# Row broadcasts of attention factors by DMA through DRAM in place of TensorE transposes, with the order picked among 45 candidates

## The chip, the cores and the metric

The kernel runs on one core of one Trainium2 chip. The metric is the device time of one execution in microseconds (us), given as the median of several runs. Each run is marked with a state, fast, slow or unknown: all timed runs told here are fast, and the two probes, which ran once each, unknown. The profile and the trace of one run of each kernel are read beside the times. Engines are PE (TensorE matmuls), PEld (TensorE weight loads), DVE (VectorE), ACT (ScalarE), POOL (GpSimd) and SP (SyncE, which here only issues DMAs). An engine with a "q" behind its name is its queue. A DMA has landed, as the word is used here, when the trace records its semaphore's event. "Granted clock" is the share of its full clock that TensorE has in the records of the profile.

## The reference, cut to what matters

There are 32 batches of `x`, each 512 rows of 256. Each goes through a layer norm, a small MLP, a first attention without a mask, a second MLP, a second attention with the mask `adj`, and then a feed-forward part that does not matter here. Both attentions are of the additive kind:

```python
def _gat(inp, adj_mask, W, a):
    h = jnp.matmul(inp, W)
    F_ = h.shape[-1]
    f1 = jnp.matmul(h, a[:F_, 0])
    f2 = jnp.matmul(h, a[F_:, 0])
    e = jax.nn.leaky_relu(f1[:, :, None] + f2[:, None, :], ALPHA)
    if adj_mask is not None:
        e = jnp.where(adj_mask[None, :, :] > 0, e, NEG_INF)
    att = jax.nn.softmax(e, axis=2)
    h_prime = jnp.einsum('bij,bjf->bif', att, h)
    return jax.nn.elu(h_prime)
```

`f1[i] + f2[j]` needs one of the two vectors as a column, one value per partition, and the other as a row, the same 512 values on all 128 partitions. The matmuls leave both as columns. How the row is made is what the change is about.

## The kernel before

In the first attention the kernel writes exp(leaky_relu(f1 + f2)) as the larger of two products of factors, so only 4 × 512 exponentials are needed (`ex`). Two of the four vectors are needed as rows (`acb`). A column becomes a row by spreading it over 128 columns and transposing that on TensorE, 128 values at a time, into PSUM, from where ScalarE copies it:

```python
        nc.vector.memset(f1, 1.0)
        acb = new("acb", [P, 2, N])
        for s in range(2):
            pt = tr_tile([P, N])
            for i in range(NT):                       # NT = 4, P = 128, N = 512
                nc.tensor.transpose(
                    pt[:, ts(i)], ex[:, s, i : i + 1].to_broadcast([P, P]), ident
                )
            nc.scalar.copy(acb[:, s, :], pt)

        pT = new("pT", [P, NT, N])
        for j in range(NT):
            nc.vector.tensor_scalar(
                pT[:, j, :], acb[:, 1, :], ex[:, 3, j : j + 1], None, op0=OP.mult
            )
            nc.vector.scalar_tensor_tensor(
                pT[:, j, :], acb[:, 0, :], ex[:, 2, j : j + 1], pT[:, j, :],
                op0=OP.mult, op1=OP.max,
            )
        # ... then the matmuls of pT with h ("mm<-h,pT")
```

The second attention does the same with one row, `f2b`, from a column of its `h`, and uses it thus:

```python
            nc.vector.scalar_tensor_tensor(
                e, f2b, h[:, i, D : D + 1], mbias[:, i, :], op0=OP.add, op1=OP.add
            )
            # ... leaky relu, row maximum, exponential, then four transposes of e on TensorE
```

No operation is issued where it is written. A `Recorder` takes all of them, gives each a cost and a lag from a small model of its own, and puts them into one order for each engine, greedily. The front of one batch (to the end of the first attention) runs beside the rest of the batch before. The model's cost of a DMA, which the change leaves as it is:

```python
        if op.method == "dma_start":
            return 0.1, 2.5 + out.size() * 4 / 180e3
```

Of the kernel before, what the change touches and what calls it, by code (L numbers as in the profile page):

```python
# [1 line left out]

# [5 lines left out]

F32 = mybir.dt.float32
# [3 lines left out]
AX = mybir.AxisListType  # L13

ENGINES = ("tensor", "vector", "scalar", "gpsimd", "sync")
LATE, LONG = 1.3, 1.4
P = 128
ALPHA = 0.2
MASKED = -4.5e16
# [2 lines left out]
class Recorder:  # L22



    SIGNAL = 0.16
    DRAIN = 0.17
    KEPT = 1
    AHEAD = 3

    def __init__(self, nc):
        self.nc, self.ops, self.logs, self.age, self.stage = nc, [], {}, -1, 0
# [2 lines left out]

    def _region(self, ap):

        if ap.space == bass.MemoryType.PSUM:
            return 0, P, 1
        (pitch, parts), *rest = ap.ap  # L40
        first, start = divmod(ap.offset, pitch)
        starts, run = [start], 1
        for step, count in rest:
            if step == 1:
                run = count
            elif step:
                starts = [s + step * i for s in starts for i in range(count)]
        bits = 0
        for s in starts:
            for w in range(s // 64, (s + run - 1) // 64 + 1):  # L50
                bits |= 1 << w
        return first, first + parts, bits

    def take(self, engine, method, args, kwargs):
        outs, ins = list(args[:1]), [x for x in args[1:] if isinstance(x, bass.AP)]
        for key, x in kwargs.items():
            if isinstance(x, bass.AP):
                (outs if key in ("out", "accum_out") else ins).append(x)
        op = _Op(engine, method, args, kwargs, self.age, self.stage, len(self.ops))
        op.cost, op.lag = self._cost(op, outs[0], ins)  # L60
        before = {}
        for aps, writes in ((ins, False), (outs, True)):
            for ap in aps:
                if ap.space == bass.MemoryType.DRAM:
                    continue
                lo, hi, bits = self._region(ap)
                log = self.logs.setdefault(ap.tensor.name, _Log(ap, self.age))
                op.logs.add(log)
                kept = []
                for entry in log.entries:  # L70
                    other, olo, ohi, obits, owrites = entry
                    if other is op:
                        kept.append(entry)
                        continue
                    if (writes or owrites) and olo < hi and lo < ohi and obits & bits:
                        before[other.index] = other
                    if not (writes and lo <= olo and ohi <= hi and not obits & ~bits):
                        kept.append(entry)
                kept.append((op, lo, hi, bits, writes))
                log.entries = kept  # L80
        for other in before.values():
            other.after.append(op)
        self.ops.append(op)
# [23 lines left out]
            return (0.1 if op.method == "memset" else 0.3 if op.method == "tensor_scalar" else 1.1), 0.1  # L107
        return 0.2 + n / (480 if op.method == "tensor_tensor" else 960), 0.1

    def _schedule(self, ops, key):  # L110


        free, slots, turn = dict.fromkeys(ENGINES, 0.0), {}, {}
# [32 lines left out]
        while len(done) < len(ops):  # L146
# [23 lines left out]
            for log in op.logs:  # L170
                users[log] -= 1
                until[log] = max(until[log], op.end)
                if not users[log]:
                    slots[log.tag].append(until[log] + self.SIGNAL)
            for later in op.after:
                if later not in left:
                    continue
                if later.engine != op.engine:
                    at = op.end + self.SIGNAL
                else:  # L180
                    at = t + op.cost if op.engine == "tensor" else op.end
                later.ready = max(later.ready, at)
# [6 lines left out]
            done.append(op)  # L189
        return done  # L190

    def order(self):


        work, turns = {}, {}
        for op in self.ops:
            stage = op.age, op.stage
            turns[op] = work.get(stage, 0.0)
            work[stage] = turns[op] + (op.cost if op.engine == "tensor" else 0.0)
        for op in self.ops:  # L200
            part = turns[op] / (work[op.age, op.stage] or 1.0)
            turns[op] = op.age + (LATE + LONG * part if op.stage else part)
        return self._schedule(self.ops, turns.get)

    def emit(self):
        for op in self.order():
# [37 lines left out]
def adj_ffn_kernel(  # L244
# [40 lines left out]
    sbuf = ctx.enter_context(tc.tile_pool(name="sbuf", bufs=1))  # L285
    psum = ctx.enter_context(tc.tile_pool(name="psum", bufs=1, space=bass.MemoryType.PSUM))

    def ts(i, n=P):
        return slice(i * n, (i + 1) * n)

# [8 lines left out]

    def sm_tile(shape):  # L300
        return psum.tile(shape, F32, tag="sm", name="sm", bufs=1)

    def med(name, shape=(P, 4, 256)):
        return new(name, shape, bufs=2, tag="med")
# [211 lines left out]
    def front(b):  # L516
# [48 lines left out]

        nc.vector.memset(f1, 1.0)
        acb = new("acb", [P, 2, N])
        for s in range(2):
            pt = tr_tile([P, N])
            for i in range(NT):  # L570
                nc.tensor.transpose(
                    pt[:, ts(i)], ex[:, s, i : i + 1].to_broadcast([P, P]), ident
                )
            nc.scalar.copy(acb[:, s, :], pt)

        pT = new("pT", [P, NT, N])
        for j in range(NT):
# [27 lines left out]
    def middle(b, o1T):  # L605
# [18 lines left out]
            else:  # L624
                nc.scalar.copy(h[:, t, :], pm)
        f2b = new("f2b", [P, N])
        pt = tr_tile([P, N])
        for j in range(NT):
            nc.tensor.transpose(pt[:, ts(j)], h[:, j, D + 1 : D + 2].to_broadcast([P, P]), ident)
        nc.scalar.copy(f2b, pt)  # L630
        r2 = new("r2", [P, NT, D])
        for t2 in range(NT // 2):
            pt = tr_tile([P, 2, D])
# [249 lines left out]
```

## Time and profile before

| | before |
|---|---|
| median | 3002.47 us (3 runs, 3002.22 to 3004.32) |
| TensorE busy | 98% |
| VectorE, ScalarE busy | 62%, 39% |
| one batch in the middle of the run | 91.28 us |
| granted clock | 0.996 |

TensorE has no time to spare, so the run is the sum of its work. The prediction shows the lines for that. One thing more of the kernel before will be needed, what VectorE waits for when it takes the rows. These are two lines of its groups by shape: busy time in all and mean ns of one, then the idle time just before them and what ended it.

```profile
L207 DVE TENSOR_SCALAR pT<-acb,ex 128x512 f32<-128x512 f32 x128 | 56.1, 481 | 3.5 <-ACT acb L207 3.5
L207 DVE SCALAR_TENSOR_TENSOR e<-f2b,h,mbias 128x512 f32<-128x512 f32 x128 | 92.9, 746 | 2.0 <-PE tr L207 1.7 <-ACT f2b L207 0.4
```

In the whole run VectorE stood idle for 3.5 us before `acb` and for 2.0 us before `e`. The rows came in time.

### The profile page before, as it was taken

To read this page: it belongs to the slowest core of one execution; us is meant where nothing else is said; L and a number is where in the kernel's file an instruction comes from. 1 tells how busy PE (TensorE), PEld (TensorE's weight loads), DVE (VectorE), ACT (ScalarE), POOL (GpSimd) and SP (SyncE) were. 2 spreads that over 40 slices of the span, in tenths; PEclk is the share of its full clock that TensorE was granted. 3 is DMA by queue.
4 is the path that set the end of the run, shared out by engine and by line. 5 is a ranking of instruction groups with operands and counts; after the bars stand their busy time and mean duration, and the time that the engine had idled before them with its cause. 6 is when DMAs were issued, how large, how long until landed. Compare 5 with 4: busy or idle time off the path is not lost.

```text
span 3002.9 us, 35910 instructions
## 1 busy us (share of the span) xinstructions
PE 2942.8 (98%) x13805; PEld 2258.5 (75%) x13805; DVE 1866.3 (62%) x4438; ACT 1174.5 (39%) x2246; POOL 124.6 (4%) x233
## 2 busy tenths in 40 slices
PE   5999999999999999999999999999999999999997
PEld 3777777877777777778777778777777777787775
DVE  3565676655775656666556756557756566665574
ACT  1433444333444334444334443334443344443342
POOL 1000000000000000000000000000000000000000
PEclk9999999999999999999999999999999999999998
DMA  4000000000000000000000000000000000000000
GB/s 130 1 22 1 21 22 22 22 9 13 22 22 22 22 1 22 22 22 22 21 1 22 22 22 22 3 19 22 22 22 22 1 22 22 22 15 13 3 15 14
DMA packets 57410, 58.71 MB, mean 20 GB/s; under 512 B 3988, under 2 KB 55832, under 8 KB 57240
## 3 DMA queue, kind: packets, MB, share of 16 engines
q1 hardware_dynamic: 53904, 54.28, 6.0%
q8 instruction: 110, 1.80, 0.3%
q10 hardware_dynamic: 3336, 2.14, 0.3%
q14 instruction: 60, 0.49, 0.1%
HBM read 39.63 MB, written 16.78 MB: 19 GB/s over the span
## 4 chain that ended last, share of the span: by engine, by line
PE 96%; DVE 2%; DMA 1%; ACT 0%; issue 0%; POOL 0%; SPq 0%; ACTq 0%; POOLq 0%
PE mm L207 84%; PE tr L207 11%; PE sm L207 1%; DVE w L207 1%; DMA wfx<-in_L_ffn_W_fx_dram 0%; DMA temp<-n_L_ffn_temperature_dram 0%; DVE mx L207 0%; DVE rs L207 0%; DVE m L207 0%; DVE u L207 0%; DMA xt<-in_x_dram 0%; ACT m L207 0%; DVE x L207 0%; POOL ln_rstd L207 0%; DVE mbias L207 0%
## 5 line engine op out<-in xcount | busy, mean ns | idle before, releaser
L207 PE MATMUL mm<-wfc,o0T 128*128 128x257 f32 x2048 | 584.5, 383 | 0.0
L207 PE MATMUL mm<-h,pT 128*128 128x256 f32 (+1 forms) x2048 | 523.6, 379 | 0.0
L207 PEld LDWEIGHTS mm<-wfc,o0T 128*128 128x128 f32 x2048 | 363.1, 190 | 117.0 <-issue 83.5
L207 PEld LDWEIGHTS mm<-h,pT 128*128 128x128 f32 x2048 | 379.9, 189 | 63.0 <-issue 13.9
L207 DVE COPY h<-mm 128x257 f32<-128x257 f32 x192 | 81.5, 425 | 378.8 <-PE mm L207 378.8
L207 PE MATMUL mm<-h,p2T 128*128 128x256 f32 x1024 | 292.6, 379 | 0.0
L207 PE MATMUL mm<-gg,wT 128*128 128x256 f32 x1024 | 281.6, 379 | 0.0
L207 PE MATMUL mm<-o1T,w 128*128 128x512 f32 x512 | 262.3, 595 | 0.0
L207 PE MATMUL mm<-xn,w 128*128 128x257 f32 x1024 | 248.2, 380 | 0.0
L207 PE MATMUL mm<-xnT,w 128*128 128x512 f32 x512 | 247.4, 598 | 0.1
L207 PE MATMUL mm<-weff,xn2T 128*128 128x512 f32 x512 | 226.9, 596 | 0.2 <-ACT xn2T L207 0.2
L207 PEld LDWEIGHTS mm<-h,p2T 128*128 128x128 f32 x1024 | 186.5, 189 | 22.7
L207 PEld LDWEIGHTS mm<-xn,w 128*128 128x128 f32 x1024 | 184.6, 190 | 20.9 <-DVE w L207 0.2
L207 PEld LDWEIGHTS mm<-gg,wT 128*128 128x128 f32 x1024 | 179.6, 190 | 17.9 <-ACT gg L207 0.2
L207 PEld LDWEIGHTS mm<-weff,xn2T 128*128 128x128 f32 x512 | 97.9, 192 | 111.0 <-issue 107.9
L207 ACT ACTIVATE w<-w 128x512 f32<-128x512 f32 x128 | 80.6, 630 | 248.0 <-DVE w L207 248.0
L207 ACT ACTIVATE m<-m 128x512 f32<-128x512 f32 x192 | 121.0, 630 | 143.8 <-DVE m L207 140.5
L207 DVE TENSOR_TENSOR w<-mm,beff 128x512 f32<-128x512 f32 x128 | 84.9, 663 | 146.1 <-PE mm L207 146.1
L207 ACT COPY h<-mm 128x257 f32<-128x257 f32 x192 | 71.8, 374 | 264.9 <-PE mm L207 264.0
L207 DVE SCALAR_TENSOR_TENSOR u<-m,u 128x512 f32<-128x512 f32 x192 | 131.9, 687 | 40.7 <-ACT m L207 38.6
L207 PE MATMUL mm<-wh,o2T 128*128 128x258 f32 x512 | 152.5, 381 | 0.0
L207 ACT ACTIVATE m<-m,neg 128x512 f32<-128x512 f32 x192 | 138.2, 720 | 5.2
(142 smaller groups left out, 4420.8 us busy)
## 6 DMA issues: line engine op xcount, KB each, us to landing
xt<-in_x_dram SPq DMA_DIRECT2D x32, 512.0 KB, 4.7
x<-in_x_dram SPq DMA_DIRECT2D x32, 512.0 KB, 4.4
out_dram<-x SPq DMA_DIRECT2D x32, 512.0 KB, 3.2
w<-in_L_gnn_mlp_w_dram SPq DMA_DIRECT2D x2, 512.0 KB, 7.6
wfc<-in_L_gnn_W_fc_dram ACTq DMA_DIRECT2D x2, 512.0 KB, 6.5
adjt<-in_adj_dram SPq DMA_DIRECT2D x1, 1024.0 KB
wfx<-in_L_ffn_W_fx_dram ACTq DMA_DIRECT2D x1, 512.0 KB, 10.0
ab<-in_L_gnn_a_fc_dram SPq DMA_DIRECT2D x1, 512.0 KB, 6.0
```

The source lines that it names most:

```text
L207: getattr(getattr(self.nc, op.engine), op.method)(*op.args, **op.kwargs)
```

## The change

The intent is to take the 12 transposes per batch from the bound engine and give the work to the DMA engines, which were nearly idle in the kernel before (their row of tenths shows 0 after the first slice). A column is written to a row in DRAM, element by element, and that row is read back into all 128 partitions at once. The order is then the best of 45 by the model's own length. Cut to its core (left out: bookkeeping of DRAM tiles in the `Recorder`, and the function that computes the length of an order):

```diff
-LATE, LONG = 1.3, 1.4
-    SIGNAL = 0.16
+    SIGNAL = 0.06
+    ORDERS = (1.0, 1.1, 1.2, 1.3, 1.4), (1.2, 1.4, 1.6), (0.0, 0.1, 0.2)
 ...
+        for late, long, spare in product(*self.ORDERS):
 ...
+            ops = self._schedule(self.ops, turns.get, spare)
+            length = self._length(ops)
+            if best is None or length < best[0]:
+                best = length, ops
 ...
+    def spread(cols, dst):
+        rows = cols.shape[1]
+        scr = dram.tile([rows, N], F32, name="scr", tag=f"row{rows}", bufs=2)
+        for s in range(rows):
+            nc.sync.dma_start(scr[s].rearrange("(t p) -> p t", p=P), cols[:, s, :])
+        nc.sync.dma_start(dst, bcast_dram(scr, rows * N))
 ...
         acb = new("acb", [P, 2, N])
-        for s in range(2):
-            pt = tr_tile([P, N])
-            for i in range(NT):
-                nc.tensor.transpose(
-                    pt[:, ts(i)], ex[:, s, i : i + 1].to_broadcast([P, P]), ident
-                )
-            nc.scalar.copy(acb[:, s, :], pt)
+        spread(ex[:, :2, :], acb.rearrange("p s n -> p (s n)"))
 ...
         f2b = new("f2b", [P, N])
-        pt = tr_tile([P, N])
-        for j in range(NT):
-            nc.tensor.transpose(pt[:, ts(j)], h[:, j, D + 1 : D + 2].to_broadcast([P, P]), ident)
-        nc.scalar.copy(f2b, pt)
+        spread(h[:, :, D + 1 : D + 2].rearrange("p t s -> p s t"), f2b)
```

More of the change, by code (lines that the diff above doesn't have):

```diff
@@ L1 @@
 from contextlib import ExitStack
+from itertools import product
 import concourse.bass as bass
@@ L5 @@
 from concourse import mybir
-from concourse.masks import make_identity
 from concourse._compat import with_exitstack
@@ L39, in _region @@
             return 0, P, 1
-        (pitch, parts), *rest = ap.ap
-        first, start = divmod(ap.offset, pitch)
+        if ap.space == bass.MemoryType.DRAM:
+            parts, first, start, rest = 1, 0, ap.offset, ap.ap
+        else:
+            (pitch, parts), *rest = ap.ap
+            first, start = divmod(ap.offset, pitch)
+        unit = 128 if ap.space == bass.MemoryType.DRAM else 64
         starts, run = [start], 1
@@ L49, in _region @@
         for s in starts:
-            for w in range(s // 64, (s + run - 1) // 64 + 1):
+            for w in range(s // unit, (s + run - 1) // unit + 1):
                 bits |= 1 << w
@@ L63, in take @@
             for ap in aps:
-                if ap.space == bass.MemoryType.DRAM:
+                if not hasattr(ap.tensor, "tag"):
                     continue
@@ L108, in _cost, with _schedule @@
         return 0.2 + n / (480 if op.method == "tensor_tensor" else 960), 0.1
-    def _schedule(self, ops, key):
+    def _schedule(self, ops, key, spare):
         free, slots, turn = dict.fromkeys(ENGINES, 0.0), {}, {}
@@ L173, in _schedule @@
                 if not users[log]:
-                    slots[log.tag].append(until[log] + self.SIGNAL)
+                    slots[log.tag].append(until[log] + self.SIGNAL + spare)
             for later in op.after:
@@ L178, in _schedule @@
                 if later.engine != op.engine:
-                    at = op.end + self.SIGNAL
+                    at = op.end + self.SIGNAL + spare
                 else:
@@ L190, in _schedule, with _length @@
         return done
+    def _length(self, ops):
+        free, ready, users, until, slots, held = {}, {}, {}, {}, {}, set()
+        for op in ops:
+            for log in op.logs:
+                users[log] = users.get(log, 0) + 1
+        for op in ops:
+            at = ready.get(op, 0.0)
+            for log in op.logs:
+                if log not in held:
+                    held.add(log)
+                    places = slots.setdefault(log.tag, [0.0] * log.bufs)
+                    places.sort()
+                    at = max(at, places.pop(0))
+            t = free.get(op.engine, 0.0)
+            t = max(t + (0.03 if op.engine == "tensor" and at > t - 0.1 else 0.0), at)
+            free[op.engine], end = t + op.cost, t + op.cost + op.lag
+            for log in op.logs:
+                users[log] -= 1
+                until[log] = max(until.get(log, 0.0), end)
+                if not users[log]:
+                    slots[log.tag].append(until[log] + self.SIGNAL)
+            for later in op.after:
+                if later.engine != op.engine:
+                    at = end + self.SIGNAL
+                else:
+                    at = t + op.cost if op.engine == "tensor" else end
+                ready[later] = max(ready.get(later, 0.0), at)
+        return max(free.values())
@@ L192, in order @@
     def order(self):
-        work, turns = {}, {}
+        work, parts = {}, {}
         for op in self.ops:
             stage = op.age, op.stage
-            turns[op] = work.get(stage, 0.0)
-            work[stage] = turns[op] + (op.cost if op.engine == "tensor" else 0.0)
-        for op in self.ops:
-            part = turns[op] / (work[op.age, op.stage] or 1.0)
-            turns[op] = op.age + (LATE + LONG * part if op.stage else part)
-        return self._schedule(self.ops, turns.get)
+            parts[op] = work.get(stage, 0.0)
+            work[stage] = parts[op] + (op.cost if op.engine == "tensor" else 0.0)
@@ new lines, in order @@
+        best = None
+        for late, long, spare in product(*self.ORDERS):
+            turns = {
+                op: op.age + (late + long * part / work[op.age, 1] if op.stage else
+                              part / (work[op.age, 0] or 1.0))
+                for op, part in parts.items()
+            }
+            try:
+                ops = self._schedule(self.ops, turns.get, spare)
+            except RuntimeError:
+                continue
+            length = self._length(ops)
+            if best is None or length < best[0]:
+                best = length, ops
@@ L205, in emit @@
+        self.length = best[0]
+        return best[1]
     def emit(self):
@@ L286, in adj_ffn_kernel @@
     psum = ctx.enter_context(tc.tile_pool(name="psum", bufs=1, space=bass.MemoryType.PSUM))
+    dram = ctx.enter_context(tc.tile_pool(name="dram", bufs=1, space=bass.MemoryType.DRAM))
     def ts(i, n=P):
```

## The prediction

> **What bounds the kernel now.** I read the page's busy shares first, then the chain that ended last, then the groups by shape, then the order of time inside one batch, then the DMA issues.
>
> ```profile
> PE 2942.8 (98%) x13805; PEld 2258.5 (75%) x13805; DVE 1866.3 (62%) x4438; ACT 1174.5 (39%) x2246; POOL 124.6 (4%) x233
> ...
> PE 96%; DVE 2%; DMA 1%; ACT 0%; issue 0%; POOL 0%; SPq 0%; ACTq 0%; POOLq 0%
> PE mm L207 84%; PE tr L207 11%; PE sm L207 1%; DVE w L207 1%; DMA wfx<-in_L_ffn_W_fx_dram 0%; DMA temp<-n_L_ffn_temperature_dram 0%; DVE mx L207 0%; DVE rs L207 0%; DVE m L207 0%; DVE u L207 0%; DMA xt<-in_x_dram 0%; ACT m L207 0%; DVE x L207 0%; POOL ln_rstd L207 0%; DVE mbias L207 0%
> ```
>
> TensorE (PE) is busy 98% of the span and 96% of the last chain, 11% of it in tiles `tr`, the transposes. The clock row shows nine tenths or more except in the last slice. So what leaves PE shortens the run, if nothing else begins to stop PE. The groups concerned:
>
> ```profile
> L207 PE MATMUL tr<-ident,ex 128*128 128x128 f32 x256 | 38.2, 273 | 0.0
> L207 PE MATMUL tr<-ident,h 128*128 128x128 f32 x128 | 24.4, 273 | 0.0
> L207 ACT COPY acb<-tr 128x512 f32<-128x512 f32 x64 | 37.4, 585 | 17.9 <-PE tr L207 17.9
> L207 ACT COPY f2b<-tr 128x512 f32<-128x512 f32 x32 | 18.8, 586 | 110.5 <-PE tr L207 110.5
> ```
>
> 256 + 128 = 384 transposes, 12 per batch of 32, and 96 ScalarE copies. The 273 ns is the length of one pipelined instruction, not what it costs. For that I read starts, in a batch from the middle:
>
> ```profile
> 1573.67 0.27 PE L207 MATMUL sm<-ident,fm 128*128 128x128 f32 x1
> ...
> 1576.39 0.60 PE L207 MATMUL mm<-gg,wT 128*128 128x256 f32 x2
> 1576.82 0.60 PE L207 MATMUL tr<-ident,ex 128*128 128x128 f32 x4
> 1577.26 0.60 PE L207 MATMUL mm<-gg,wT 128*128 128x256 f32 x2
> 1577.69 0.60 PE L207 MATMUL tr<-ident,ex 128*128 128x128 f32 x4
> 1578.13 2.32 PE L207 MATMUL mm<-gg,wT 128*128 128x256 f32 x10
> ...
> 1581.59 1.03 PE L207 MATMUL mm<-h,pT 128*128 128x257 f32 x4
> ```
>
> From the start of four transposes to the next start is 0.44 us, 0.109 us each; the busy sums of the groups (38.2 and 24.4) share out overlap and are no price either. One batch repeats every 91.28 us (the same run of 44 matmuls starts at 2638.89 and 2730.17). `fm` is the transpose that opens the factors' chain; the factors `ex` are ready on ScalarE 1.9 us later (its exponential starts at 1575.33 and takes 0.22). The first matmul that uses the factors, `h,pT`, starts 7.9 us after `fm`.
>
> The DMA lines that I size the new transfers from:
>
> ```profile
> x<-in_x_dram SPq DMA_DIRECT2D x32, 512.0 KB, 4.4
> out_dram<-x SPq DMA_DIRECT2D x32, 512.0 KB, 3.2
> ...
> setup<-in_L_ffn_W_v_dram SPq DMA_DIRECT2D x2, 16.0 KB, 2.0
> ...
> bxc<-in_L_ffn_b_x_dram ACTq DMA_DIRECT2D x1, 2.0 KB, 7.4
> ```
>
> In mid-run the DMA engines are nearly idle (the row of DMA tenths shows 0 after the first slice), so bandwidth is free; latency is the question. `bxc` is the one of the change's kind, 512 separate elements of 4 bytes, but its 7.4 us are spent behind megabytes of weights.
>
> [...] Each column write is thus 512 packets of 4 bytes. The trace's packet records agree for loads: `bxc` moved its 512 packets in about 1.1 us once its turn came. No DRAM write of 4 bytes is in this trace, so what such a write costs at its end I can't size.
>
> **The change, part by part.** It removes 384 transposes: 384 × 0.109 = 41.9 us of PE time. All of it is on the path, as PE has no gaps there. It removes 96 copies of 0.586 us from ScalarE (56 us, off the path: 39% busy). It adds, for each batch, two column writes and a 512 KB broadcast (`acb`), one column write and a 256 KB broadcast (`f2b`): 160 DMAs more, all on SyncE's queue. And it reorders everything: a lower assumed signal time, and the best by its own model among 5 × 3 × 3 orders.
>
> I counted the work that stands in PE's queue in the new order, with the spacings of the trace (0.857 us for two passes of 512 columns, 0.433 for 256, 0.109 for a transpose). The whole queue falls from 2910.4 to 2868.7 us, the same 41.7. In the middle of the run, 12.67 us of other PE work now stand between `fm` and the first `h,pT`, in place of 7.9; and 13.85 us between the last matmul of the second attention's `h` and the first transpose of its `e`, in place of 9.64, which puts these transposes 19.2 us after `fm`. So the scheduler knows of the latency and puts work before it. The start is the same list up to the first `fm`, and the last batch's serial tail is made of the same parts, so I give neither a change.
>
> **Does the latency fit?** Times from `fm`. The factors are there at 1.9. Column writes: the 512 KB store lands in 3.2 us, of which 512 packets at 46 ns (their mean in the packet records) over 16 engines are 1.5, so 1.7 is fixed; 512 elements are 1.1 us; the pair, issued 0.4 apart (`bxc`'s issue took 0.39), lands after 3.2 us if they overlap, 4.3 if they queue. The broadcast: 4.4 less 1.5 gives 2.9 fixed, plus 8 packets of 4 KB per engine at 0.16 to 0.25 us (the `ab` broadcast's in the packet records), 1.3 to 2.0: 4.2 to 4.9. With 0.1 for handing on, `acb` lands at 1.9 + 0.1 + 3.2 to 4.3 + 4.2 to 4.9 = 9.4 to 11.2, in the middle 10.3.
>
> What it must meet: VectorE makes the first piece of pT in some 1.5 us (two scalings at 0.4, one combination at 0.66), so PE's 12.67 needs `acb` by about 11.0. On VectorE's queue the rows of `e` now stand behind all eight pT instructions: 4.3 us of these, then 3.2 us to the first row maximum, then 0.9 for ScalarE's exponential; PE's 19.2 needs `acb` by about 10.6. So it fits by 0.3 us in my middle estimate, and misses by 0.6 at the late end. `f2b` has more room: its column is ready near 6.2, and write plus broadcast (2.8 + 3.6) end near 13, before VectorE gets to it at 14.
>
> Sum: 3002.5 − 41.8 = 2960.7. For the share of cases in which `acb` is late I add an average of 0.3 us per batch, 10 us; for a better packing I take off some 8. That makes 2963.
>
> **Rivals.** *The DMA chain takes the place of the transposes.* Each microsecond by which `acb` misses stops a PE that has no spare time, so it costs 32 us. A miss of 1.3 us eats the whole gain; 3.2 us makes the kernel 2% slower. For it: two latencies in series, unknown 4-byte DRAM writes, 128 readers of the same 4 KB. Against it: an idle DMA system, and a budget of 12.67 us that the scheduler left on purpose. If the elements take twice the time that they took as loads, the pair is 2 us later and the run is near 3005 to 3020. *The order gives more than the transposes.* PE starts in ten periods of the middle that come later than the usual spacing of their shape sum to 6.6 us, so 0.66 per batch, 21 in all. If the new order closes all of it: 2940. For it: the choice among 45. Against: the old order was good already, and the choice is made by a model that knows neither packets nor queues. *The transfer is late but hidden, and something else shows:* `out`, `xt` and `x` stand after the broadcasts in SyncE's queue, so they go some 10 us later in the period; they have about 90 us, so I expect nothing. *VectorE becomes the bound:* it waits some 6 us more per batch before pT, but at 62% it has 35 us; it can only show through the 10.6 above.
>
> **Range and chances.** No stall and some packing: 2945 to 2962, about half of the cases. A stall of up to 0.8 us: 2962 to 2988, about a third. More: the rest. Faster by over 2% needs less than 2942.4, the whole of the gaps beside the transposes: 0.04. Slower by over 2% needs a miss above 3.2 us: 0.05. Eight in ten: 2947 to 2993.
>
> **What would show it.** Transposes of `ex` and `h` gone, and the middle period at 89.5 to 90.2 us. Two writes before `acb` landing in 3 to 4.5 us from the first issue, `acb` in 4.2 to 4.9. Waits of PE for pT, or for `e`, near nothing. I am wrong if PE's weight loads wait for VectorE's pT or for the `e` chain by more than 1 us in each batch while VectorE waits for the DMA of `acb`; if the period stays at 91; or if the start or the tail moves by over 10 us.

## The result

| | before | after |
|---|---|---|
| median (4 runs each) | 3003.39 us (3002.22 to 3004.86) | 3430.18 us (3429.15 to 3430.32) |
| one batch (median of the distances from batch to batch) | 91.28 us | 104.54 us |
| granted clock | 0.996 | 0.941 |
| time at half clock in the trace | 23.5 us | 406.4 us |

The ratio is 1.142 (95% interval 1.140 to 1.144): the kernel became 14% slower. Ratios are the mean time of one kernel's fast runs over that of the other's of the same rounds, so they are not quite the ratios of the medians quoted.

The page first: busy shares, then the chain that ended last by engine.

```profile
PE 3073.7 (90%) x13421; PEld 2302.3 (67%) x13421; DVE 1863.4 (54%) x4438; ACT 1102.2 (32%) x2150; POOL 112.6 (3%) x233
...
PE 65%; DMA 22%; DVE 9%; ACT 3%; issue 1%; SPq 0%; ACTq 0%; POOL 0%; DVEq 0%; POOLq 0%
```

The 384 transposes are gone (13805 to 13421 instructions). PE is down from 98% to 90% of a longer span, and yet its busy time rose, from 2942.8 to 3073.7 us, with less to do: so its instructions took longer. The chain is now DMA for 22%, where it was 1%. The groups of VectorE that take the rows show where, in the columns of the two lines before:

```profile
L255 DVE TENSOR_SCALAR pT<-acb,ex 128x512 f32<-128x512 f32 x128 | 56.3, 482 | 280.4 <-DMA acb<-scr 280.4
L255 DVE SCALAR_TENSOR_TENSOR e<-f2b,h,mbias 128x512 f32<-128x512 f32 x128 | 93.0, 748 | 187.6 <-DMA f2b<-scr 184.4
```

The instructions are as fast as before (482 and 748 ns). VectorE waits 280.4 us for `acb` and 184.4 us for `f2b` that it did not wait for. The DMA issues tell which of the two legs is long (KB each, then the median us from issue to landing):

```profile
acb<-scr SPq DMA_DIRECT2D x32, 512.0 KB, 4.4
...
f2b<-scr SPq DMA_DIRECT2D x32, 256.0 KB, 4.4
...
scr<-ex SPq DMA_DIRECT2D x64, 2.0 KB, 8.6
...
scr<-h SPq DMA_DIRECT2D x32, 2.0 KB, 10.2
```

The broadcasts of 256 and 512 KB take 4.4 us. The column writes, 2 KB each, take 8.6 and 10.2. This is one batch on SyncE's queue (start, duration of the issue, queue, line, what, how many) and on PE (the bracket is idle time before and what ended it):

```profile
1583.11 0.92 SPq L255 DMA_DIRECT2D scr<-ex  x2
...
1592.18 0.33 SPq L255 DMA_DIRECT2D acb<-scr  x1
1592.62 0.37 SPq L255 DMA_DIRECT2D scr<-h  x1
...
1602.78 0.33 SPq L255 DMA_DIRECT2D f2b<-scr  x1
```

```profile
1580.89 0.27 PE L255 MATMUL sm<-ident,fm 128*128 128x128 f32 x1
...
1592.70 1.02 PE L255 MATMUL mm<-xnT,w 128*128 128x512 f32 x2
1598.55 6.54 PE L255 MATMUL mm<-h,pT 128*128 128x257 f32 x16 [4.82 <-DVE pT L255]
...
1610.78 0.86 PE L255 MATMUL tr<-ident,e 128*128 128x128 f32 x4 [1.16 <-ACT e L255]
```

Three things are to be seen here.

First, the writes of `ex` are issued at 1583.11, and the packet records have all their elements sent within about 0.9 us, from 1584.01 to 1584.93 (1056 packets of 4 bytes for the two writes: 512 elements each, and 16 more for each DMA); but `acb`, which needs them landed, goes out only at 1592.18. PE has used up its other work before `acb` has landed, and stops for 4.82 us.

Second, the column of the second attention was ready at 1587.27 (the end of ScalarE's and VectorE's copies of its `h`). Its write was not issued before 1592.62. SyncE issued in the order of its queue here: it stood at `acb`, waiting for the first writes, until 1592.18, and the write behind stood with it, for 5.35 us. In the packet records its elements were then sent only from 1595.92 on; the packets of the `acb` broadcast, issued just before it, start from 1593.89 to 1596.40.

Third, the 16 passes of `h,pT` after the stop take 6.54 us. At the usual spacing of 0.216 us they take 3.46. The windows of this batch show why (stretch, its length, busy time of PE, PEld, DVE, ACT, POOL with instructions, PEclk, DMA share, GB/s):

```profile
1598.50:1605.10 6.60, 6.55 (x17) 5.24 (x18) 2.77 (x5) 0.00 (x0) 0.00 (x0) 0.56 0.07 9
1605.10:1610.70 5.60, 3.27 (x12) 1.82 (x11) 3.89 (x8) 1.84 (x5) 0.00 (x0) 1.00 0.17 36
1610.70:1615.00 4.30, 4.22 (x14) 3.52 (x15) 4.16 (x9) 2.93 (x7) 0.00 (x0) 0.60 0.59 176
```

The granted clock is 0.56 in the stretch after the stop, and again 0.60 after the next stretch, in which PE was busy for only 3.27 of 5.60 us, waiting for the late `e`. By the trace's records the clock stood at exactly one half from 1597.44 to 1604.26, which is 6.83 us, and from 1611.09 to 1614.5. In the whole trace 60 of the 61 stretches at half clock last 3.41, 6.83 or 10.24 us, one, two or three times the same length (the last one 3.58), so I looked at the 3.41 us before each fall. Before the first fall here, inside the stop of 4.82 us, PE stood idle for the whole 3.41. Before the second, in the 3.41 us up to 1611.09, it stood idle for 2.4 us, in two stops: so the clock also fell where PE was not wholly idle. Over the whole run the clock fell to one half 61 times. In the 3.41 us before each fall PE had been idle for 1.91 us or more in all cases but one (0.96, in the last batch), and in none of the 813 windows of that length that left the clock full was it idle for more than 1.75. So in this trace some 1.9 us idle of 3.41 went before nearly every fall. The trace of told, below, does not fit this limit: 27 of its 99 falls came after less than 1.91 us, so what sets the fall is not shown.

### The profile page after: what moved, and what is told of

It reads as the page before. It is cut to its first block, busy times and chain, and to the rows that moved or that the text cites. A ratio compares the mean times of both kernels' runs of the same rounds, so it can differ in the third digit from the quotient of the medians.

```text
span 3428.5 us, 35357 instructions
## 1 busy us (share of the span) xinstructions
PE 3073.7 (90%) x13421; PEld 2302.3 (67%) x13421; DVE 1863.4 (54%) x4438; ACT 1102.2 (32%) x2150; POOL 112.6 (3%) x233
## 4 chain that ended last, share of the span: by engine, by line
PE 65%; DMA 22%; DVE 9%; ACT 3%; issue 1%; SPq 0%; ACTq 0%; POOL 0%; DVEq 0%; POOLq 0%
PE mm L255 56%; DMA scr<-h 9%; DMA scr<-ex 8%; PE tr L255 8%; DMA f2b<-scr 4%; DVE u L255 2%; DVE e L255 2%; ACT m L255 1%; PE sm L255 1%; DMA acb<-scr 1%; DVE ln_st L255 1%; DVE w L255 1%; DVE m L255 1%; ACT e L255 1%; DVE x L255 1%
## 5 line engine op out<-in xcount | busy, mean ns | idle before, releaser
L255 PE MATMUL mm<-h,pT 128*128 128x257 f32 (+1 forms) x2048 | 641.7, 444 | 244.1 <-DVE pT L255 192.9
L255 PEld LDWEIGHTS mm<-h,pT 128*128 128x128 f32 x2048 | 444.6, 226 | 365.9 <-DVE pT L255 211.3
L255 PE MATMUL mm<-wfc,o0T 128*128 128x257 f32 x2048 | 565.9, 383 | 0.6 <-ACT u L255 0.6
L255 ACT ACTIVATE u<-mm,rd 128x256 f32<-128x256 f32 x192 | 90.4, 471 | 585.0 <-DVE rd L255 446.5
L255 PE MATMUL mm<-gg,wT 128*128 128x256 f32 x1024 | 267.6, 381 | 0.0
L255 PEld LDWEIGHTS mm<-h,p2T 128*128 128x128 f32 x1024 | 199.2, 200 | 29.5 <-ACT p2T L255 0.8
L255 DVE TENSOR_SCALAR pT<-acb,ex 128x512 f32<-128x512 f32 x128 | 56.3, 482 | 280.4 <-DMA acb<-scr 280.4
L255 DVE SCALAR_TENSOR_TENSOR e<-f2b,h,mbias 128x512 f32<-128x512 f32 x128 | 93.0, 748 | 187.6 <-DMA f2b<-scr 184.4
L255 DVE COPY h<-mm 128x257 f32<-128x257 f32 (+1 forms) x192 | 80.9, 422 | 152.3 <-PE mm L255 151.9
L255 ACT COPY h<-mm 128x257 f32<-128x257 f32 (+1 forms) x192 | 72.0, 375 | 239.5 <-PE mm L255 236.7
```

The lines of the kernel that those rows point to most:

```text
L255: getattr(getattr(self.nc, op.engine), op.method)(*op.args, **op.kwargs)
```

## The experiments

They ran in four groups, each beside the kernel before on the same chip (its medians there lie between 3002.6 and 3004.51 us). All outputs were correct. The theory to be tested: the small writes land late because of their form, SyncE's queue carries this on to the second row, and the clock makes each stop dearer. The rivals: the number of packets or any DRAM write is slow; the sharing of one queue does nothing; the new order is bad by itself; the clock only shows what the waits already cost.

| run | median us | ratio to before (95%) |
|---|---|---|
| probe (one run) | 3001.96 | |
| probe2 (one run) | 3002.22 | |
| acb_only | 3247.85 | 1.0811 (1.0795 to 1.0828) |
| f2b_only | 3253.72 | 1.0831 (1.0813 to 1.0849) |
| h_on_act | 3275.65 | 1.0911 (1.0896 to 1.0926) |
| acb_only_warm | 3149.39 | 1.0483 (1.0467 to 1.0498) |
| order_only | 3003.25 | 0.9996 (0.9979 to 1.0013) |
| told | 4623.18 | 1.5362 (1.5269 to 1.5455) |
| told2 | 2980.07 | 0.9921 (0.9907 to 0.9935) |
| packed | 3039.81 | 1.0119 (1.0104 to 1.0134) |
| packed_pe | 3035.10 | 1.0104 (1.0089 to 1.0119) |
| packed_act | 2992.62 | 0.9964 (0.9950 to 0.9977) |
| packed_act_told | 2977.11 | 0.9913 (0.9900 to 0.9927) |
| packed_act_wide | 2964.04 | 0.9868 (0.9852 to 0.9885) |

### What makes the small write slow: probe and probe2

Both are the kernel before with one more DMA per batch, whose result nobody uses. The form of it changes from batch to batch, so one run measures them all with the DMA engines nearly idle (their row of tenths shows 0 after the first slice in probe and in probe2).

```diff
+        col, form = ex[:, 0, :], "abcdefhik"[b % 9]
+        if form == "a":      # 512 x 4 bytes into one packed row: the change's write
+            nc.sync.dma_start(dst("pa", [N]).rearrange("(t p) -> p t", p=P), col)
+        elif form == "b":    # the same elements, 64 bytes apart
+            nc.sync.dma_start(dst("pb", [N, 16])[:, 0].rearrange("(t p) -> p t", p=P), col)
+        elif form == "c":    # 512 bytes apart
+            nc.sync.dma_start(dst("pc", [N, 128])[:, 0].rearrange("(t p) -> p t", p=P), col)
+        elif form == "d":    # 128 pieces of 16 bytes
+            nc.sync.dma_start(dst("pd", [P, NT]), col)
+        elif form == "f":    # 128 x 4 bytes, packed
+            nc.sync.dma_start(dst("pf", [P, 1]), col[:, 0:1])
 ...                         # e: pieces of 32 bytes; h: two of a; i: 16-byte pieces 64 bytes apart; k: a load
```

> The kernel before, with one extra DMA per batch that nobody waits for, in nine forms in turn, each measured from issue to landing. Forms: a = 512 elements of 4 bytes into one packed row in DRAM (the change's write); b = the same 512 elements, each 64 bytes from the next in DRAM; c = each 512 bytes from the next; d = 128 pieces of 16 bytes, packed; e = 128 pieces of 32 bytes, packed; f = 128 elements of 4 bytes, packed; h = two of a, one behind the other; i = 128 pieces of 16 bytes, 64 bytes apart; k = a load of 512 elements of 4 bytes from DRAM. Theory (many tiny writes that share the same short stretch of DRAM finish slowly, after their packets were long sent): a near 8, h near 8.5 to 9, d, e, i and k below 4, f between, b and c clearly shorter than a. Rival 1 (it is the number of elements, wherever they go): a, b and c alike near 8, f a quarter of the way, k as long as a. Rival 2 (any write to DRAM lands late when it is issued in mid-run): d, e, f and i near 8 too. The time of the kernel stays within 0.5% of before in all cases, since nobody waits.

The median landing of four of the forms:

```profile
pa<-ex SPq DMA_DIRECT2D x4, 2.0 KB, 8.7
pb<-ex SPq DMA_DIRECT2D x4, 2.0 KB, 1.8
...
pd<-ex SPq DMA_DIRECT2D x4, 2.0 KB, 1.4
...
pf<-ex SPq DMA_DIRECT2D x3, 0.5 KB, 7.7
```

The change's write takes 8.7 us where nobody waits for it, so it is no matter of the kernel after. The same 512 elements 64 bytes apart take 1.8, and 512 bytes apart 2.0: the count of packets is not what costs, nor is 4 bytes as such. A quarter of the elements, packed, still takes 7.7: I had expected this between the two and was wrong. The load of 512 elements of 4 bytes took 2.1, so loads of this form are not slow. Two writes together took 8.9, hardly more than one.

The second probe takes the steps between "packed" and "64 bytes apart", and one form in which neighbours in DRAM come from neighbouring partitions in another way.

```diff
+        sp = {"a": 1, "b": 2, "c": 4, "d": 8}.get(form)     # elements from one write to the next
+        if sp:
+            nc.sync.dma_start(dst("q" + form, [N, sp])[:, 0].rearrange("(t p) -> p t", p=P), col)
+        else:                                               # e: 4 neighbouring partitions fill 64 bytes
+            nc.sync.dma_start(dst("qe", [P, NT]), ex[:, 0:NT, 0])
```

> The kernel before with one unused DMA per batch again, in five forms. a = 512 elements of 4 bytes packed into one row (8.7 us before); b, c and d = the same with 8, 16 and 32 bytes from one element to the next; e = 512 elements of 4 bytes, packed, in an order in which every 64 consecutive bytes come from four neighbouring partitions. Theory (the writes into one 64-byte stretch are done one after another, each some 0.45 us, whoever sends them): a 8.7, b near 5, c near 3.2, d near 2.2 (1.8 and 0.46 for each further writer), e as slow as a. Rival (only writes from different DMA engines into one stretch get in each other's way[...]): e near 2, and a to d as above. Rival 2 (a threshold: any packing below 64 bytes is slow): b, c and d all near 8.

| distance of the 4-byte writes | 4 | 8 | 16 | 32 | 64 bytes (probe) |
|---|---|---|---|---|---|
| writers in 64 bytes | 16 | 8 | 4 | 2 | 1 |
| landing, us | 9.4 | 4.2 | 2.7 | 1.9 | 1.8 |

Form e, also 16 writers in 64 bytes, but from four partitions, took 8.3. The time grows from 1.8 us with one writer to 9.4 with 16, and from 8 to 16 it more than doubles. What costs in these runs is 4-byte writes that fall close together, from 16 partitions or from four. One thing stays open: four pieces of 16 bytes also share 64 bytes, and they took 1.4 us. I have no run that tells why those are free.

### Each row alone: acb_only and f2b_only

Each undoes one half of the change: the transposes come back for the other row.

```diff
# acb_only
-        spread(h[:, :, D + 1 : D + 2].rearrange("p t s -> p s t"), f2b)
+        pt = tr_tile([P, N])
+        for j in range(NT):
+            nc.tensor.transpose(pt[:, ts(j)], h[:, j, D + 1 : D + 2].to_broadcast([P, P]), ident)
+        nc.scalar.copy(f2b, pt)
# f2b_only: the same for acb in place of f2b
```

> The changed kernel with f2b made by TensorE transposes as before, and only the first attention's rows through DRAM (order picked again by its own model: 14.8 us of PE work between fm and the first matmul on pT). Theory: from fm, the factors at 2.2, the writes 8.7, the broadcast 4.4 and the first pT 1.5 come to 17.2 us or so, 2.4 late in every batch: 3003 - 28 + 77 = 3050, range 3000 to 3120. If what the two spreads lose simply adds, this loss and that of f2b_only sum to the 427 us of the change; if SyncE's queue makes the one wait for the other, they sum to clearly less.

> The changed kernel with the first attention's factors by TensorE transposes as before, and only f2b through DRAM (13.0 us of PE work between the last matmul of its h and the first transpose of e). Theory: 0.7 for the copy of h, 8.3 for the write with nothing before it in SyncE's queue, 4.2 for the broadcast and 3.1 for the first row of e come to 16.3, so 3.3 late: 3003 - 14 + 106 = 3095, range 3040 to 3150. If the 10.2 us of this write in the changed kernel came from the broadcast of acb beside it, it lands in 8.3 or less here; if not, it stays at 10.

Both came out slower than expected: 244 us over the kernel before for `acb` alone, 250 for `f2b` alone. By the test that I had set, the two losses sum to the whole, 427 us, if they simply add, and to less if the queue couples them. They sum to 494, which fits neither. Two things were left out: the stop is longer than I had reckoned (2.4 us for `acb` alone), and the clock makes it dearer. PE in one batch of the first:

```profile
1527.94 3.79 PE L255 MATMUL mm<-h,pT 128*128 128x257 f32 x8 [5.38 <-DVE pT L255]
```

The stop is 5.38 us. Eight passes then take 3.79 in place of about 1.9, and the records hold 232.8 us at half clock over the run, 7.3 per batch. Each of these kernels has another order, so their difference says nothing certain of the shared queue. One reading does help: the column write of `h`, which landed in 10.2 us beside `acb`, lands in 8.6 when alone.

### The shared queue: h_on_act

The column of `h` is written through ScalarE's queue. Nothing else in the code changes (the order on PE differs in 233 of 13421 places).

```diff
-    def spread(cols, dst):
+    def spread(cols, dst, queue=None):
 ...
-            nc.sync.dma_start(scr[s].rearrange("(t p) -> p t", p=P), cols[:, s, :])
+            (queue or nc.sync).dma_start(scr[s].rearrange("(t p) -> p t", p=P), cols[:, s, :])
 ...
-        spread(h[:, :, D + 1 : D + 2].rearrange("p t s -> p s t"), f2b)
+        spread(h[:, :, D + 1 : D + 2].rearrange("p t s -> p s t"), f2b, nc.scalar)
```

> The changed kernel, same PE order, with one DMA moved: the write of the second attention's column is issued from ScalarE's queue, so it need not wait until SyncE's queue has seen the first write land. In the changed kernel it stood ready some 5 us before SyncE issued it. Theory (part of the loss is the two slow writes one after the other in SyncE's queue): the column lands 5 to 6 us earlier, period 103 to about 98, time 3230 to 3300. Rival (the first spread alone sets the loss): within 1% of the changed kernel's 3430.

This hit: 3275.65 us. The issues on SyncE's queue in one batch:

```profile
1612.68 0.92 SPq L255 DMA_DIRECT2D scr<-ex  x2
...
1621.75 0.33 SPq L255 DMA_DIRECT2D acb<-scr  x1
1625.45 0.33 SPq L255 DMA_DIRECT2D f2b<-scr  x1
```

The write of `h` went out on ScalarE's queue at 1616.92, 4.8 us before `acb`, and `f2b` follows `acb` by 3.70 us, not by 10.60 as after the change. So 3430.18 − 3275.65 = 154 us of the loss came from one queue that waits in order (with what follows from it: the write itself now lands in 8.7 us, where it took 10.2 behind `acb`), and the time at half clock fell from 406.4 to 255.9 us with it. The first stop is still there.

### Is the clock a cost of its own: acb_only_warm

If the half clock is only a sign of the stop, filling the stop with useless work gains nothing. If it costs of itself, it gains. The edit puts 11 matmuls on constants before the first `h,pT` of each batch of acb_only. They write a PSUM tile that the next matmul overwrites.

```diff
+    WARM = 11
 ...
+            if op.method == "matmul" and op.args[1].tensor.tag.startswith("pT_") and op.age not in seen:
+                seen.add(op.age)
+                for _ in range(self.WARM):
+                    self.nc.tensor.matmul(op.args[0], *self.filler, start=True, stop=True)
 ...
+    nc.filler = ident, wfc[:, 0, 0, :]
```

> acb_only (3248 us, period 98.96), and in each batch 11 useless matmuls (4.8 us) stand directly before the first matmul on pT, into the PSUM tile that this matmul then starts anew, so that TensorE works through the 5.4 us in which it waits. Nothing waits less for the DMAs. Theory (each stop costs twice: the wait, and some 6.8 us at half clock after it, worth 3.4): the stretches at half clock go, the period falls by about 3.4 to 95.5, and the time by about 100 us to 3130 to 3170, though TensorE has 152 us more work. Rival (waiting alone; the half clock falls on time that is waited anyway): 3235 to 3260.

```profile
1570.87 4.93 PE L261 MATMUL mm<-wfc,ident 128*128 128x257 f32 x22
1575.81 2.00 PE L262 MATMUL mm<-h,pT 128*128 128x257 f32 x8
```

The eight passes take 2.00 us in place of 3.79. The time at half clock fell from 232.8 to 20.7 us, and the kernel became 98 us faster, with 152 us of useless work added (32 × 4.76 us, from the spacing). The estimate from the records is near: if half of the time at half clock is lost, as the 3.79 and 2.00 us of the eight passes suggest, it is (232.8 − 20.7) / 2 = 106 us. So the stop is paid twice, as a wait and as slow work afterwards, about 3.1 us per batch.

### The order: order_only, told and told2

order_only has the change's ordering (45 candidates, the lower signal time) and both rows by transposes.

```diff
# on the kernel after
-        spread(ex[:, :2, :], acb.rearrange("p s n -> p (s n)"))
-        spread(h[:, :, D + 1 : D + 2].rearrange("p t s -> p s t"), f2b)
+        ...  (both rows as in the kernel before)
```

> The changed kernel with both spreads put back to TensorE transposes: what is left of the change is the choice among 45 orders and the signal time of 0.06 us. Theory (the order choice is worth at most the 0.66 us of gaps in each batch, 21 us in all): 2985 to 3005. Rival (the choice itself is bad, and part of the loss is its): above 3020.

It is the same as before (0.9996). With the rows made by transposes, the choice among 45 neither costs nor gives anything.

told gives the model the landings that the trace after showed, so that the scheduler can plan for them.

```diff
         if op.method == "dma_start":
-            return 0.1, 2.5 + out.size() * 4 / 180e3
+            if out.space == bass.MemoryType.DRAM and hasattr(out.tensor, "tag"):
+                return 0.45, 8.5
+            return 0.35, 4.3
```

> The changed kernel, with nothing changed but two constants of its scheduler's DMA model: a write into the DRAM row is given 8.5 us until it has landed, every other DMA 4.3 us. It finds an order with 53 us of PE work between fm and the first matmul on pT (12.7 in the changed kernel). Theory (the loss is a latency that the order did not allow for; DMA and SyncE have time enough): the writes still take 8.6 to 10 us and nobody waits for them; period 89.7 to 90.5, time 2950 to 2980. Rival (the DMA traffic or SyncE's queue costs PE time by itself): above 3010.

It missed wholly, at 4623.18 us, with 1047.9 us at half clock. The 45 orders give the back of a batch its turn 1.0 to 1.4 batches after its front, and none of them seems to fit latencies this long. This run says nothing on whether the latency can be hidden. told2 therefore widens the search, and is otherwise the same:

```diff
-    ORDERS = (1.0, 1.1, 1.2, 1.3, 1.4), (1.2, 1.4, 1.6), (0.0, 0.1, 0.2)
+    ORDERS = (1.2, 1.4, 1.6, 1.8, 2.0, 2.2), (1.2, 1.6, 2.0, 2.4), (0.0, 0.2)
```

> As told (the scheduler is told 8.5 us for a write into the DRAM row and 4.3 for other DMAs), with a wider choice of how far the second half of a batch may lag behind its first. The order found has 18.6 us of PE work between fm and the first matmul on pT (needed by the chip's times: 2.2 + 8.9 + 4.4 + 1.5 = 17.0), and 21.9 between the last matmul of the second h and the first transpose of e (needed: some 16.8). Theory (the loss is a latency that the order did not allow for, and told failed only because none of its 45 orders could hold it): writes still 8.6 to 10 us, period 89.6 to 90.5, time 2950 to 2985. Rival (slow writes cost PE time even where nobody waits for them): above 3020.

It came to 2980.07 us, 0.8% faster than the kernel before, while the writes are as slow as ever:

```profile
scr<-ex SPq DMA_DIRECT2D x64, 2.0 KB, 8.6
```

In one batch in its middle 18.6 us of other work stand between `fm` and the first `h,pT`, where the kernel after has 12.67. So the slow write is a latency: with an order that has room for it the loss is gone, and 22.5 us of the 41.7 that the transposes took are gained. How much of these 22.5 comes from the wider search itself is not known.

### The write in pieces of 16 bytes: packed and packed_pe

Since the 16-byte pieces land in 1.4 us, one may write all values of a partition as one piece. The row then lies in another order (partition first), and someone must pick its elements with a stride. In packed it is VectorE, where it reads `acb` and `f2b`:

```diff
-        scr = dram.tile([rows, N], F32, name="scr", tag=f"row{rows}", bufs=2)
-        for s in range(rows):
-            nc.sync.dma_start(scr[s].rearrange("(t p) -> p t", p=P), cols[:, s, :])
+        scr = dram.tile([P, rows * NT], F32, name="scr", tag=f"row{rows}", bufs=2)
+        nc.sync.dma_start(scr, cols.rearrange("p s t -> p (s t)"))
 ...
+        ac = [acb[:, :, s, :].rearrange("q p t -> q t p") for s in range(2)]
 ...   # pT and e read ac and f2b in this way; the column of h is first copied to a small tile
```

> The changed kernel with the same PE order, but the factors go to DRAM as one write of 128 pieces of 32 bytes (and the second attention's column, after a small copy that packs it, as 128 pieces of 16 bytes); the row then stands in another order, and VectorE reads it with a stride. Theory (512 four-byte writes are what lands late): the write lands in under 3.5 us in place of 8.6, both broadcasts come before PE needs them, the period falls from 103 to about 90 us, and the time is 2955 to 2985. Rival (a write to DRAM and a read back is slow whatever its pieces): write still near 8 us, time above 3300. Rival (SyncE's queue in order is the main cause): time between 3100 and 3300.

The writes landed in 1.4 us and the loss of 427 us shrank to 36, with nearly the order on PE that the kernel after has (628 of 13421 places differ). This confirms the cause. But the expected 2955 to 2985 was missed, for VectorE pays for the stride:

```profile
scr<-ex SPq DMA_DIRECT2D x32, 4.0 KB, 1.4
...
L255 DVE SCALAR_TENSOR_TENSOR e<-f2b,h,mbias 128x512 f32<-128x512 f32 x128 | 145.7, 1162 | 5.7 <-DMA f2b<-scr 5.2 <-PE tr L255 0.5
L255 DVE SCALAR_TENSOR_TENSOR pT<-acb,ex,pT 128x512 f32<-128x512 f32 x128 | 140.6, 1144 | 0.0
```

The first line is the write, of both rows at once. The two instructions took 746 and 748 ns before, now 1162 and 1144; DVE is 22% of the last chain, 2% before. The steps here are 16 bytes in `f2b` and 32 in `acb`. No run has a smaller step, so whether a smaller one costs this too is not shown.

In packed_pe the stride is left to TensorE, which reads the finished `pT` and `e` in that order, on the theory that it reads its 128 columns at any step:

```diff
-                        pm, pT[:, j, ts(i)], h[:, j, s, : HH + 1 - s],
+                        pm, pT[:, j, :].rearrange("q (p t) -> q t p", t=NT)[:, i, :], h[:, j, s, : HH + 1 - s],
 ...
-                nc.tensor.transpose(pt[:, j, :], e[:, ts(j)], ident)
+                nc.tensor.transpose(pt[:, j, :], e.rearrange("q (p t) -> q t p", t=NT)[:, j, :], ident)
```

> As packed (one write per spread, in pieces of 16 bytes per partition and row), but VectorE reads and writes contiguously (mask and factors kept in the transposed order), and the stride is in what TensorE reads: its weights from pT and the blocks of e that it transposes. Theory (packed lost its gain to strided VectorE reads, 0.68 and 1.15 us in place of 0.48 and 0.75, 12 of them in each batch): with those back at 0.48 and 0.75 and weight loads still near 190 ns, period near 90 and time 2950 to 2975. Rival (TensorE's strided reads cost as much): weight loads of pT well above 216 ns, time above 3050.

The rival held in its weight loads, though the time is below the 3050 that it named. At 3035.10 us the kernel is about the same as packed:

```profile
L255 PEld LDWEIGHTS mm<-h,pT 128*128 128x128 f32 x2048 | 520.4, 323 | 32.5 <-PE mm L255 6.9 <-DVE pT L255 5.3 <-issue 2.2
```

A weight load of `pT` takes 323 ns where it took 189. The matmuls that use them start 0.233 us apart in the trace, where it was 0.216; for 2048 of them that is 35 us, and TensorE is the engine that bounds the kernel. The writes, here two rows of 16-byte pieces, landed in 2.2 and 2.0 us.

### A version that beats both: packed_act, packed_act_told, packed_act_wide

ScalarE is busy 32% of the time after the change. It can bring the rows into order, as it did with the copies from PSUM before:

```diff
# on packed's write
+        acr = new("acr", [P, P, 2, NT])
+        spread(ex[:, :2, :], acr.rearrange("q p s t -> q (p s t)"))
+        for s in (1, 0):
+            nc.scalar.copy(acb[:, s, :].rearrange("q (t p) -> q t p", p=P),
+                           acr[:, :, s, :].rearrange("q p t -> q t p"))
 ...   # the same for f2b; pT and e as in the kernel before
```

> As packed, but VectorE reads contiguously again: after each broadcast ScalarE copies the row into the old order (three copies of 512 per batch, as many as it made from PSUM before). Theory: writes 1.4 us, broadcasts 3.6, ScalarE copies 0.6 to 1.0 each, and VectorE's pT and e back at 0.48 and 0.75; PE waits for little: 2960 to 2990. Rival (reordering costs the gain wherever it is done): 3020 to 3040 like packed and packed_pe.

2992.62 us, just outside what was expected, and for the first time under the kernel before on this path. A strided copy takes 1.13 us (0.585 from PSUM before), so `acb` comes later than the model believes. packed_act_told gives the model the landings that were measured (1.4 for the writes, 4.0 for other DMAs):

```diff
-            return 0.1, 2.5 + out.size() * 4 / 180e3
+            if out.space == bass.MemoryType.DRAM and hasattr(out.tensor, "tag"):
+                return 0.35, 1.4
+            return 0.35, 4.0
```

> As packed_act, and the scheduler is told what the packed DMAs take (1.4 us for a write, 4.0 for the rest), so that it puts 10.7 us of PE work between fm and pT and 13.2 before e. Theory: no more than 0.5% from packed_act, 2950 to 2990. Rival (the true times leave too little room for what the model of SyncE and of ScalarE's strided copies leaves out): slower than packed_act by over 1%.

2977.11 us. packed_act_wide adds the wider search of told2, with three values for the spare time:

```diff
-    ORDERS = (1.0, 1.1, 1.2, 1.3, 1.4), (1.2, 1.4, 1.6), (0.0, 0.1, 0.2)
+    ORDERS = (1.2, 1.4, 1.6, 1.8, 2.0, 2.2), (1.2, 1.6, 2.0, 2.4), (0.0, 0.1, 0.2)
```

> packed_act_told with the wider choice of orders of told2 (13.5 us of PE work between fm and pT, 13.3 before e). Theory (the 41.8 us are there, and what packed_act_told lacks of them is in gaps of its order and in the start and the end): 2955 to 2972. Rival (period stays at 90.3 and start and end as they are): 2973 to 2980.

2964.04 us (2962.90 to 2966.67), a hit, 1.3% faster than the kernel before and the fastest of all runs. The kernel before on this chip has 3004.51, so 40 us are gained, near the 41.8 that the transposes are worth. But the two need not be the same microseconds. Its middle period is 90.40 us, 0.88 less than the 91.28 before, where 12 transposes are worth 1.31: over 32 batches that is 28 us, and the other 12 lie at the start and the end of the run. The period is much as in packed_act (90.48), so most of the 28.6 us between these two lies at the start and the end too. I did not run the wider search with the transposes, so how much of the 40 us it would give to the kernel before is not known.

## Why the prediction was wrong

**The step that failed** is this term of the sum: "Column writes: … the pair, issued 0.4 apart … lands after 3.2 us if they overlap, 4.3 if they queue." It measured 8.6. It was put together from a 4-byte load's time per element and the fixed part of a 512 KB store. Both were right for what they are (the load took 2.1 us in the probe), but neither is a store of packed 4-byte elements, and the packets were indeed sent in 0.9 us. What I took for the cost, the packets, is not the cost; the landing is. The prediction said that such a write's end "I can't size", and then sized it with a spread of 1.1 us. That sentence should have widened the range: the chance of 0.05 for a miss above 3.2 us had no measurement behind it.

**The budget.** With 8.7 us from the first issue to the landing of the pair in place of 3.2 to 4.3, the way to `acb` follows the prediction's own sum. The factors were ready 2.2 us after `fm` (1.9 predicted), the broadcast took 4.4 (4.2 to 4.9 predicted), handing on took 0.5 in the batch shown (0.37 from the landing of the pair to the issue of `acb`, 0.10 from the landing of `acb` to VectorE; 0.1 predicted), `acb` was in use at 16.1 us (9.4 to 11.2 predicted, about 11.0 needed), and the first `h,pT` came at 17.7 against the 12.67 of work that stood before it: 5.0 late, and PE idle for 4.82 of them. The first rival, the DMA chain in place of the transposes, named just this wait. Its mechanism was right and its size off: it allowed for twice the time of the elements, 3005 to 3020 us.

**"`f2b` has more room"** also failed. It reckoned the write of `h` from the time when its column is ready. That write stood in the queue behind `acb`'s wait for the first writes, for 5.35 us in the batch shown, then took 10.2 us; VectorE got to `e` at 25.9 us, where 14 was planned. h_on_act puts 154 us on the place of this write in the queue. It needed the slow first writes: had they landed after 3.2 to 4.3 us, at 1586.3 to 1587.4, the queue would have been free at about the time when the column was ready (1587.27).

**"Each microsecond … costs 32 us"** holds only while the clock stays full. One of 5.4 us in acb_only cost some 3 us more per batch, by the clock (98 us in acb_only_warm). The whole loss is an estimate from these numbers: against 3003.4 − 41.7 = 2961.7 us the kernel after loses 468; half of the added time at half clock, (406.4 − 23.5) / 2 = 191 us, is slow work after stops (at most: of the 6.83 us shown 1.11 still lie in the stop), and the other 277 us, 8.7 per batch, are the stops and what is left over. The batch shown has stops of 4.82, 1.25 and 1.16 us.

**What held, and what stays open.** PE lost 384 transposes at a spacing of 0.109 us. That the run is shorter by all of it where nothing stops PE is not shown: packed_act_wide comes to 2964, where 2960.7 was reckoned, but its period fell by 0.88 us only, to 90.40, outside the 89.5 to 90.2 foretold (that of told2, 90.22, lies at the upper end). VectorE did not become the bound after the change; where the stride was put on it, it took 22% of the last chain. The second rival, that the order gives more than the transposes, fell: order_only gives nothing. "I am wrong if PE's weight loads wait for VectorE's pT … while VectorE waits for the DMA of `acb`" is what the trace showed.

## What to carry to other kernels

Measure a small DMA in the form in which it will run, to its landing, before planning with it: here the same 2 KB took 1.4 us in 16-byte pieces and 8.7 as packed 4-byte elements, and a probe in one run would have told. Give the scheduler measured landings and enough orders to choose from, and put DMAs that wait for one another on different queues if something else stands behind them (154 us here). With TensorE as the bound, a stop of 5.38 us in acb_only cost about 3.1 us per batch beyond its length, by the half clock that came with it; in the kernel after, short stops close together (2.4 us in 3.41) were also followed by 3.41 us at half clock.
